# Layer 0 of a four-layer graph network: four gather slots a row, the excess packed over partitions, packing turned round

## The chip, the cores and the metric

The kernel runs on one core of a Trainium2 chip. Its five engines work side by side, each through its own queue in order: TensorE (PE) multiplies matrices, VectorE (DVE) works on rows, ScalarE (ACT) evaluates functions, GpSimd (POOL) here issues indirect DMAs (gathers), SyncE (SP) issues loads. Sixteen DMA engines[...] move data between the large memory (HBM) and the on-chip SBUF; PE writes its sums into PSUM. The metric is the device time of one launch in microseconds, median over the runs.

## The reference, cut to what matters

There are 4096 nodes with 64 features and a 0/1 adjacency with a chance of 1/1024 for each entry, so a row has about four neighbours. Each of four layers adds its output to `x`, on a normalized and rectified copy `h`. Layer 0, which the change concerns, is hyperbolic attention:

```
adj_att = sigmoid(left[:, None] + right[None, :] + b_att) * adj
x_local = logmap(h[:, None, :], h[None, :, :], c)         # per pair (i, j)
support = einsum('ij,ijd->id', adj_att, x_local)
x = x + proj(expmap(h, support, c), c)
```

Only pairs with an edge count, some 16,600 of 16.8 million. Layers 1 and 2 are dense products of the adjacency with features (one, then two), and layer 3 weights each row's last 100 neighbours by powers of one half. These are done as dense matmuls.

## The kernel before, in words

`neighbours` does layer 0, `layers123` the rest. A dense version, `general`, stands behind a flag: it runs only if a row or partition has more neighbours than the lists hold, which these inputs do not.

**Stream.** The adjacency (64 MiB of fp32) comes in 64 pieces of 1 MiB (`load`, L597), eight to a block of 512 rows, through three buffers. From each piece ACT makes an fp8 copy (L774 for the first three blocks, which stay in SBUF; L777 for the others, which go to HBM and come back when layer 1 begins, L1251), and PE packs the bits: 16 adjacency bits of a column become one exactly represented number, with the bit pattern of the piece as the stationary side and an 8-column matrix of powers of two as the moving side (L782). `keys` then holds for each row 256 words with their word numbers in the low bits (added by a matmul of `ones1` and `word_b`, L765; copied by ACT, L788).

**Lists** (`lists`, DVE). For each of the four 128-row tiles of a block the 16 largest words are found (L815 to L817), unpacked into up to 48 candidates, and the `NS` = 7 largest become the row's gather slots (`idx`). What is beyond (`rem`) is collected over 16 tiles; for each partition the `NO` = 12 largest leftovers of such a half are listed with their owners.

**Gathers** (POOL, L890). One indirect DMA fetches one table row (`rows_d`: `h`, its norm terms, the right half of the attention) for each of 128 partitions: 7 for a tile, and for each half 12 neighbours (`es_o`) and 12 owners (`hi_o`).

**Sums.** `chunk` forms the products of neighbours and own rows (L918, L919), `weights` the attention and logmap factor, `sums` scales (L1011) and adds the slots by matmuls with the identity (L1014). `more_sums` spreads each leftover over the tiles of its half, with products on DVE and ACT (L1029, L1027) and 192 matmul records (L1032). `finish` does expmap and projection, eight tiles at a time (L1060 to L1141).

**Order.** All is in a schedule written out by hand: `units_at` says how many pieces to pack at each of 34 items (32 tiles, two overflows), `begin` when lists start, `after` when sums do; `portion` takes turns between the two. Each engine executes in the order of the program.

Of the kernel before, what the change touches and what calls it, by code (L numbers as in the profile page):

```python
# [17 lines left out]
P = 128  # L18
N = 4096
# [23 lines left out]
NS = 7  # L43
GRP = 8
SUP = 16
NO = 12
DQ = D + 1
TW = D + 4
# [526 lines left out]
def neighbours(ctx, tc, x_in, x, sh, adj_t, adj8, a8, over):  # L575
# [5 lines left out]

    nc = tc.nc
# [11 lines left out]
    def load(b, v):  # L594
# [12 lines left out]
    p32_f = l0.tile([P, 1], F32, name="p32_f")  # L607
    G.iota(p32_f, pattern=[[0, 1]], base=0, channel_multiplier=NCH, allow_small_or_imprecise_dtypes=True)
    io16 = l0.tile([P, SUP], F32, name="io16")
    G.iota(io16, pattern=[[1, SUP]], base=1, channel_multiplier=0, allow_small_or_imprecise_dtypes=True)  # L610

    word_b = l0.tile([1, NCH, 8], BF16, name="word_b")
    G.iota(word_b, pattern=[[1, NCH], [NCH, 8]], base=0, channel_multiplier=0, allow_small_or_imprecise_dtypes=True)
    ones1 = l0.tile([1, P], BF16, name="ones1")
    V.memset(ones1, 1.0)

    noff = l0.tile([P, SUP, 16], F32, name="noff")
    G.iota(
        noff, pattern=[[2 * N, SUP], [0, 16]], base=1 - 127 * NCH, channel_multiplier=0,
# [5 lines left out]
    pc_f = l0.tile([P, 1], F32, name="pc_f")  # L625
    cc = l0.tile([P, 8], F32, name="cc")
    wpack = l0.tile([P, 8], BF16, name="wpack")
# [3 lines left out]
    V.tensor_scalar(cc, io16[:, :8], pc_f, None, op0=ALU.is_equal)  # L631
    V.tensor_scalar(pr_i, pr_i, 127 + 8, None, op0=ALU.add)
    V.tensor_scalar(pr_i, pr_i, 23, None, op0=ALU.logical_shift_left)
    V.tensor_scalar_mul(wpack, cc, pr_i.bitcast(F32))
# [49 lines left out]
    left = l0.tile([P, NCH], F32, name="left")  # L684
# [13 lines left out]
    def row_stage(beside):  # L698

        st, var, right = row("st"), row("var"), row("right")  # L700
# [12 lines left out]
        for m in range(NQ):  # L713
            beside()
            V.tensor_mul(cens[m], cens[m], bc(inv[:, rows_of(m)], D))
            S.activation(h[:, rows_of(m), :], cens[m], AF.Relu)
            sq, sr = block(f"sqx{m}"), block(f"sqr{m}")
            S.activation(sq, h[:, rows_of(m), :], AF.Square)
            G.tensor_mul(sr, h[:, rows_of(m), :], sh.wr_t[:, None, :].to_broadcast([P, 8, D]))
            V.tensor_reduce(x2[:, rows_of(m)], sq, AX.X, ALU.add)  # L720
            V.tensor_reduce(right[:, rows_of(m)], sr, AX.X, ALU.add)
            G.tensor_mul(cens[m], h[:, rows_of(m), :], sh.wl_t[:, None, :].to_broadcast([P, 8, D]))
# [15 lines left out]
        V.tensor_scalar(tab[:, :, D + 3], pn, NOISE2, RSQRT_MIN, op0=ALU.mult, op1=ALU.add)  # L738
        V.tensor_sub(la, la, lb)
        V.scalar_tensor_tensor(la, tcl, -2.0, la, op0=ALU.mult, op1=ALU.add)  # L740
        V.tensor_mul(la, la, iv)
        V.tensor_mul(tab[:, :, D + 2], right, la)
        nc.scalar.dma_start(rows_d[1:, :].rearrange("(p n) w -> p n w", p=P), tab)
        return la, cens

    def row_rest(att, cens):
        for m in range(NQ):
            V.tensor_reduce(left[:, rows_of(m)], cens[m], AX.X, ALU.add)
        V.tensor_mul(left, left, att)
        V.tensor_scalar_add(left, left, sh.batt_t)  # L750

        V.tensor_scalar(beta, x2, negc_t, 1.0, op0=ALU.mult, op1=ALU.add)
        V.tensor_scalar_max(clipb, beta, MIN_NORM)
# [4 lines left out]
    def pack(u):  # L758

        b, part = divmod(u, 2)  # L760
        if part == 0:
            keys[b] = l0w.tile([P, 4, NW], F32, tag="keys", bufs=3, name=f"keys{b}")
        pk = psum.tile([P, 4, 16, 8], F32, tag="k", bufs=2, name=f"pk{u}")
        chunks = slice(part * 16, part * 16 + 16)
        T.matmul(  # L765
            pk.rearrange("p k j w -> p k (j w)"), ones1,
            word_b[:, None, chunks, :].rearrange("p k j w -> p k (j w)").to_broadcast([1, 4, 128]),
            start=True, stop=False, skip_group_check=True,
        )
        for v in range(4):  # L770
# [8 lines left out]
            bits = a.bitcast(BF16).rearrange("p j (k i b) -> p j k i b", k=4, b=2)  # L779
            for j in range(4):  # L780
                for k in range(4):
                    T.matmul(  # L782
                        pk[:, k, 4 * v + j, :], bits[:, j, k, :, 1], wpack,
                        start=False, stop=(v == 3 and j == 3), skip_group_check=True,
                    )
            if v < 3:
                yield
        S.copy(keys[b][:, :, part * 128 : part * 128 + 128], pk.rearrange("p k j w -> p k (j w)"))  # L788
# [3 lines left out]
    LB = 4  # L792
# [3 lines left out]
    ovx = [l0.tile([P, NO], U32, name=f"ovx{v}") for v in range(2)]  # L796
    own = [l0.tile([P, NO], U32, name=f"own{v}") for v in range(2)]
    mks = [l0.tile([P, NO], F32, name=f"mk{v}") for v in range(2)]
    rems = {}

    def lists(nb):
        sup, k0 = divmod(nb * LB, SUP)
        nl = LB

# [3 lines left out]
        if k0 == 0:  # L808
            rems[sup] = l0w.tile([P, SUP, 48], F32, tag="rem", name=f"rem{sup}")
        rem = rems[sup]  # L810
        k16 = tile_("k16", [nl, 16])
        scr = tile_("scr", [NW])
        for k in range(nl):
            kk = keys[nb][:, k, :]
            V.max(k16[:, k, :8], kk)  # L815
            V.match_replace(scr, k16[:, k, :8], kk, 0.0)
            V.max(k16[:, k, 8:], scr)  # L817
            yield 1.25
# [5 lines left out]
        ki, wi = tile_("ki", [nl, 16], I32), tile_("wi", [nl, 16], I32)  # L824
        wf, vf = tile_("wf", [nl, 16]), tile_("vf", [nl, 16])
        V.tensor_copy(ki, k16)
        V.tensor_scalar(wi, ki, NW - NCH, 4, op0=ALU.bitwise_and, op1=ALU.logical_shift_left)
        V.tensor_add(wf, wi, noff[:, k0 : k0 + nl, :])
# [6 lines left out]
        cand = tile_("cand", [nl, 3, 16])  # L835
# [9 lines left out]
        j8 = tile_("j8", [nl, 8])  # L845
        for k in range(nl):
# [3 lines left out]
        ji = tile_("ji", [nl, NS], I32)  # L850
# [4 lines left out]
        cr, rm = cand.rearrange("p k l w -> p k (l w)"), rem[:, k0 : k0 + nl, :]  # L855
        V.tensor_tensor(rm, cr, j8[:, :, NS - 1 : NS].to_broadcast([P, nl, 48]), op=ALU.is_lt)
        V.tensor_mul(rm, rm, cr)
        yield 0.9
        if k0 + nl < SUP:
            return  # L860

        ov = l0e.tile([P, 16], F32, tag="ov", name=f"ov{sup}")
        ovm, of = (l0e.tile([P, NO], F32, tag=t, name=f"{t}{sup}") for t in ("ovm", "of"))
        oi, oj = (l0e.tile([P, NO], I32, tag=t, name=f"{t}{sup}") for t in ("oi", "oj"))
        rf = rem.rearrange("p k w -> p (k w)")
        V.max(ov[:, :8], rf)
        yield 1.0
        V.match_replace(rf, ov[:, :8], rf, 0.0)
        yield 1.0
        V.max(ov[:, 8:], rf)  # L870
        V.tensor_copy(flags[:, nb, 2:3], ov[:, NO : NO + 1])
        yield 1.2
        V.tensor_copy(oi, ov[:, :NO])
        V.tensor_scalar(ovm, ov[:, :NO], 0.0, None, op0=ALU.is_gt)
        V.tensor_scalar(oj, oi, 2 * N - 1, None, op0=ALU.bitwise_and)
        yield 0.5
        V.tensor_scalar_min(ovx[sup], oj, N)
        V.tensor_scalar(oj, oi, 13, None, op0=ALU.logical_shift_right)
        V.scalar_tensor_tensor(mks[sup], oj, 1.0, ovm, op0=ALU.add, op1=ALU.mult)
        yield 0.5  # L880
        V.tensor_scalar(of, mks[sup], p32_f, float(SUP * sup), op0=ALU.add, op1=ALU.add)
        V.tensor_mul(of, of, ovm)
        V.tensor_scalar_min(own[sup], of, float(N))
        yield 0.5


    es, s_e, es_o, hi_o, s_o, on_o, w_o = {}, {}, {}, {}, {}, {}, {}
# [6 lines left out]
    def gather(item):  # L894
        kind, n = item
        if kind == "tile":
            g, k = divmod(n, GRP)
            if k == 0:
                es[g] = l0w.tile([P, GRP, NS, TW], F32, tag="es", name=f"es{g}")
            for s in range(NS):  # L900
                fetch(es[g][:, k, s, :], idx[n // LB][:, n % LB, s : s + 1])
            return
        es_o[n] = l0e.tile([P, NO, TW], F32, tag="es_o", name=f"es_o{n}")
        hi_o[n] = l0e.tile([P, NO, TW], F32, tag="hi_o", name=f"hi_o{n}")
        for s in range(NO):
            fetch(es_o[n][:, s, :], ovx[n][:, s : s + 1])
        for s in range(NO):
            fetch(hi_o[n][:, s, :], own[n][:, s : s + 1])

    def chunk(item):  # L910

        kind, n = item
        if kind == "tile":
            g, k = divmod(n, GRP)
            if k == 0:
                s_e[g] = l0w.tile([P, GRP, NS], F32, tag="s_e", name=f"s_e{g}")
            pd = block(f"pd{n}")[:, :NS, :]
            V.tensor_mul(pd, es[g][:, k, :, :D], h[:, n, None, :].to_broadcast([P, NS, D]))  # L918
            V.tensor_reduce(s_e[g][:, k, :], pd, AX.X, ALU.add)  # L919
            return  # L920
        s_o[n] = l0e.tile([P, 1, NO], F32, tag="s_o", name=f"s_o{n}")
        pd = l0e.tile([P, NO, D], F32, tag="pd_o", name=f"pd_o{n}")
# [690 lines left out]
```

## Time and profile before

| | us |
|---|---|
| median of 3 runs | 1254.74 (1245.7 to 2050.95) |
| profiled execution, span | 1141.5 |
| PE busy | 653.3 |
| DVE busy | 547.0 |
| ACT busy | 383.9 |
| POOL busy | 277.3 |

Busy times are sums over the span; the stages differ in what limits them, so each is to be read by itself. A group row gives line, engine, operation, output and input with shapes and a count, then busy time and the mean of one in ns, then the engine's idle time ahead of it and what ended that. A stage row gives busy time and number of instructions of each engine, PE's granted clock (1 is full), the mean busy share of the 16 DMA engines, and GB/s.

### The profile page before, as it was taken

The page shows a single profiled execution, that of the slowest core. Times are in us where ns is not written, and L with a number is a line of the kernel's source. Part 1 is how long each engine was busy: PE and PEld are TensorE (multiplying, and loading weights), DVE is VectorE, ACT ScalarE, POOL GpSimd, SP SyncE. Part 2 cuts the span into 40 slices and gives each one's busy share as a digit, 9 for nine tenths or more (in the row PEclk, how much of TensorE's full clock was granted, in tenths as well). Part 3 has the DMA queues.
Part 4 walks back from the last instruction along what each step waited for, and adds up shares of the span by engine and source line. Part 5 has one row for each costly group of instructions (what it writes and reads, how often), then busy time and mean ns, then how long its engine had stood idle before and what let it go on. Part 6 is the DMA issues. An engine that isn't in the chain of part 4 may idle for free.

```text
span 1141.5 us, 15854 instructions
## 1 busy us (share of the span) xinstructions
PE 653.3 (57%) x6266; PEld 533.8 (47%) x6266; DVE 547.0 (48%) x1599; ACT 383.9 (34%) x576; POOL 277.3 (24%) x290
## 2 busy tenths in 40 slices
PE   1111141033361310434158999899899689999997
PEld 1111030022251210323058999899899556656564
DVE  4762463076848661675643554222244434444443
ACT  4754354036446410533321111111122234334343
POOL 0377765477371766600000000000000000000000
PEclk9999985566575655766569999899999889999999
DMA  8899989857749548200620000000000000000000
GB/s 293 267 312 242 237 246 248 112 119 189 219 118 322 154 20 27 24 0 1 256 113 1 2 1 2 1 1 2 1 2 1 1 1 1 10 1 11 10 1 13
DMA packets 51813, 102.25 MB, mean 90 GB/s; under 512 B 8082, under 2 KB 8082, under 8 KB 50834
## 3 DMA queue, kind: packets, MB, share of 16 engines
q1 hardware_dynamic: 35232, 79.70, 19.9%
q0 software_dynamic: 8704, 9.49, 11.8%
q10 hardware_dynamic: 7794, 11.97, 2.8%
q8 instruction: 51, 0.84, 0.3%
q14 instruction: 32, 0.26, 0.1%
HBM read 88.47 MB, written 12.65 MB: 89 GB/s over the span
## 4 chain that ended last, share of the span: by engine, by line
PE 51%; DVE 15%; DMA 11%; POOL 10%; ACT 6%; issue 6%; ACTq 0%; DVEq 0%; POOLq 0%
PE l2a_acc L1326 8%; PE l_acc L1326 8%; POOL es L890 8%; PE l2b_acc L1326 8%; PE l_acc L1447 7%; PE cnt L1471 6%; PE cnt L1460 5%; DMA hi_o<-rows_d,own 4%; DMA a<-in_adj_t 4%; PE v L1032 4%; PE v L1014 3%; DMA es<-rows_d,idx 2%; POOL es_o L890 2%; ACT f L777 1%; PE l_u L1287 1%
## 5 line engine op out<-in xcount | busy, mean ns | idle before, releaser
L1326 PEld LDWEIGHTS <-a 128*128 128x128 fp8e4 x3072 | 264.4, 99 | 12.5 <-issue 10.5
L890 POOL DMA_INDIRECT es<-rows_d,idx x224 | 219.7, 981 | 132.7 <-issue 86.5
L782 PE MATMUL pk<-wpack,a 128*128 128x8 bf16 x1024 | 36.5, 168 | 196.2 <-DMA a<-in_adj_t 196.2
L1467 DVE TENSOR_SCALAR wt<-cnt 128x512 int16<-128x512 f32 x128 | 88.5, 692 | 122.0 <-PE cnt L1460 122.0
L1468 ACT ACTIVATE wt<-cnt,low_t 128x512 int16<-128x512 f32 x128 | 87.9, 687 | 136.8 <-PE cnt L1460 136.8
L782 PEld LDWEIGHTS <-a 128*128 128x128 bf16 x1024 | 32.0, 103 | 208.0 <-DMA a<-in_adj_t 205.7
L1032 PE MATMUL v<-vo,ident 128*128 128x260 f32 x192 | 55.3, 446 | 113.2 <-DVE vo L1029 109.1
L1447 PE MATMUL l_acc<-y_b,wt 128*128 128x192 bf16 x1024 | 107.2, 248 | 0.0
L1447 PEld LDWEIGHTS <-wt 128*128 128x128 bf16 x1024 | 89.7, 98 | 31.7 <-issue 2.5
L1032 PEld LDWEIGHTS v<-vo,ident 128*128 128x128 f32 x192 | 41.0, 222 | 126.3 <-DVE vo L1029 110.3
L1326 PE MATMUL l_acc<-y_a,a 128*128 128x193 bf16 x1024 | 93.8, 251 | 3.6 <-DVE y_a L1296 3.6
L777 ACT CAST f<-a 128x2048 fp8e4<-128x2048 f32 x40 | 75.8, 1894 | 54.3 <-DMA a<-in_adj_t 49.6
L1014 PE MATMUL v<-es,ident 128*128 128x260 f32 x112 | 40.7, 538 | 88.7 <-DVE es L1011 78.2
L1326 PE MATMUL l2a_acc<-y_b,a 128*128 128x192 bf16 x1024 | 89.1, 249 | 2.9 <-DVE y_b L1296 2.9
L1326 PE MATMUL l2b_acc<-y_a,a 128*128 128x192 bf16 x1024 | 88.1, 248 | 3.0 <-DVE y_a L1296 3.0
L1471 PE MATMUL cnt<-a,fill 128*128 128x512 fp8e4 x248 | 81.3, 384 | 11.1 <-DVE wt L1467 11.1
L1460 PE MATMUL cnt<-a,tri 128*128 128x512 fp8e4 x256 | 78.4, 388 | 9.6 <-DVE tri L1440 9.6
L1014 PEld LDWEIGHTS v<-es,ident 128*128 128x128 f32 x112 | 30.3, 278 | 96.5 <-DVE es L1011 89.6
L774 ACT CAST a<-a 128x2048 fp8e4<-128x2048 f32 x24 | 45.3, 1894 | 31.5 <-DMA a<-in_adj_t 29.9
L1027 ACT ACTIVATE vo<-es_o,on 128x65 f32<-128x65 f32 x128 | 32.8, 337 | 64.0 <-PE v L1032 61.3
L1460 PEld LDWEIGHTS <-tri 128*128 128x128 bf16 x256 | 24.8, 97 | 47.0 <-issue 22.1
L923 DVE TENSOR_TENSOR pd_o<-es_o,hi_o 128x768 f32<-128x768 f32 x2 | 1.9, 966 | 79.6 <-DMA es<-rows_d,idx 79.6
(333 smaller groups left out, 799.1 us busy)
## 6 DMA issues: line engine op xcount, KB each, us to landing
a<-in_adj_t SPq DMA_DIRECT2D x64, 1024.0 KB, 9.5
adj<-f ACTq DMA_DIRECT2D x40, 256.0 KB, 6.6
a<-adj SPq DMA_DIRECT2D x5, 2048.0 KB, 21.5
es<-rows_d,idx POOLq DMA_INDIRECT x224, 6.0
rows_d<-tab ACTq DMA_DIRECT2D x1, 1088.0 KB, 4.7
x<-in_x SPq DMA_DIRECT2D x1, 1024.0 KB
out<-z SPq DMA_DIRECT2D x4, 256.0 KB, 2.0
es_o<-rows_d,ovx POOLq DMA_INDIRECT x24, 7.7
```

Of the source, the lines that this page charges most:

```text
L774: S.copy(a8[b][:, 4 * at : 4 * at + 4, :], a, saturate=False)
L777: S.copy(f8, a, saturate=False)
L782: T.matmul(pk[:, k, 4 * v + j, :], bits[:, j, k, :, 1], wpack, start=False, stop=(v == 3 and j == 3), skip_group_check=True,)
L890: G.indirect_dma_start(out=dst, out_offset=None, in_=rows_d, in_offset=bass.IndirectOffsetOnAxis(ap=at, axis=0))
L1014: T.matmul(pv, sh.ident, es[g][:, 4 * q : 4 * q + 4, s, :DQ], start=(s == 0), stop=False, skip_group_check=True,)
L1032: T.matmul(banks[g][:, half, : 4 * DQ], sh.ident, vo[:, 4 * q : 4 * q + 4, :].rearrange("p k e -> p (k e)"), start=False, stop=(s == NO - ...
L1326: T.matmul(acc, a8[n // 4][:, c, n % 4 * P : (n % 4 + 1) * P], y3[:, c, :cols], start=(c == first[0] and k % 2 == 0), stop=(c == last[-1] ...
L1447: T.matmul(accs[k // 2][:, k % 2, : 3 * D], wts[k // 4][:, (k % 4) * P : (k % 4 + 1) * P].bitcast(BF16), y3[:, c, : 3 * D], start=(c == NC ...
L1460: T.matmul(cnt[b], tri, masks[b], start=head_, stop=last, skip_group_check=True)
L1467: V.tensor_scalar(wts[0], cnt[0], -(128.0 - MAX_NEIGH) * UNIT, 0.0, op0=ALU.add, op1=ALU.max)
L1468: S.activation(wts[1], cnt[1], AF.Relu, bias=low_t)
L1471: T.matmul(cnt[b], fill, masks[b], start=False, stop=False, skip_group_check=True)
```

## The change

Layer 0 is written anew on the same idea.

- A row has four slots instead of seven. What is beyond is no longer kept with its own partition: within each block, every partition lists up to 24 leftovers (`NV`), a matmul with a strict triangle (`before`) counts those of the partitions ahead of it, and a second matmul with a 0/1 matrix (`mine`) moves each leftover to its place in a list of 4 × 128 (`NO`). So a block needs 16 + 4 neighbour gathers and 4 owner gathers.
- A leftover's contribution is added to its row by a matmul with a 0/1 matrix (`spot`), in place of `more_sums`.
- Packing has the adjacency as moving side: 4 matmuls of 512 columns for a piece, with 128-column windows of a wide `wpack` as stationary side. The result lies with words on partitions, so ACT adds the numbers as a bias and PE transposes each 128 × 128 part into `keys`, which is in PSUM now.
- The table row has one word more (the left half of the attention), so this is computed before the table is written.
- The order comes from a loop that keeps a clock of its own: it packs a piece when it should have arrived, runs lists before anything else, then products of blocks whose gathers should have landed, then sums and finishes.
- In the later layers, the triangle masks of layer 3 are made before layer 1, one product is placed two chunks earlier, and a buffer count is written as an expression.

```diff
-NS = 7
-GRP = 8
-SUP = 16
-NO = 12
+NS = 4
+LB = 4
+NV = 24
+NO = 4
-TW = D + 4
+TW = D + 5
...
-            keys[b] = l0w.tile([P, 4, NW], F32, tag="keys", bufs=3, name=f"keys{b}")
-        pk = psum.tile([P, 4, 16, 8], F32, tag="k", bufs=2, name=f"pk{u}")
+            keys[b] = [psum.tile([P, 2, NW], F32, tag="k", bufs=2, name=f"keys{b}_{s}") for s in range(2)]
+        pk = psum.tile([P, 512], F32, tag="pk", bufs=2, name=f"pk{u}")
...
             for j in range(4):
-                for k in range(4):
-                    T.matmul(
-                        pk[:, k, 4 * v + j, :], bits[:, j, k, :, 1], wpack,
-                        start=False, stop=(v == 3 and j == 3), skip_group_check=True,
-                    )
+                w = 4 * v + j
+                T.matmul(
+                    pk, wflat[:, w * P : (w + 1) * P], bits[:, j, :, 1], start=(w == 0), stop=(w == 15),
+                )
...
+        kt = l0w.tile([P, 512], F32, tag="kt", name=f"kt{u}")
+        S.activation(kt, pk, AF.Identity, bias=num[:, part : part + 1])
+        for k in range(LB):
+            T.transpose(
+                keys[b][k // 2][:, k % 2, part * P : part * P + P], kt[:, k * P : (k + 1) * P], sh.ident
+            )
...
+        for v in range(0, NV, 8):
+            V.max(ov[:, v : v + 8], rf)
+            if v + 8 < NV:
+                V.match_replace(rf, ov[:, v : v + 8], rf, 0.0)
...
+        T.matmul(pb[:, :1], before, cnb, start=True, stop=True)
...
+        V.tensor_scalar(from_, io, at0, None, op0=ALU.is_gt)
+        V.tensor_add(end, at0, cnt)
+        V.scalar_tensor_tensor(mine, io, end, from_, op0=ALU.is_le, op1=ALU.mult)
...
+        for c in range(NO):
+            T.matmul(pe[:, c, :], mine[:, c * P : (c + 1) * P], mv, start=True, stop=True, skip_group_check=True)
...
+            for c in range(NO):
+                V.tensor_scalar(spot[:, c, :], io, rows_at[nb][:, c : c + 1], None, op0=ALU.is_equal)
+                yield 0.4
+            ek = es[g][:, q, :, :DQ]
+            V.tensor_mul(ek, ek, bc(w[:, q - q0, :], DQ))
...
+            for c in range(NO):
+                for k in range(LB):
+                    T.matmul(
+                        pv[:, k * DQ : (k + 1) * DQ], spot[:, c, k * P : (k + 1) * P],
+                        es[g][:, q, LB * NS + c, :DQ], start=False, stop=(c == NO - 1 and k == LB - 1),
+                        skip_group_check=True,
+                    )
...
+    PACE_MB, PACE_DMA, LANDED, SLOW = 3.6, 1.27, 8.0, 1.1
...
+        def can_pack():
+
+            b, v = divmod(packed[0], 8)
+            return b < NR and (v < 3 or turned[0] >= b)
...
+        arrived = [38.0 + PACE_MB * (m - 8) for m in range(8 * NR)]
...
+        follow = {
+            1: [sums(0, 0, 2), finish(0, 0, 8)],
+            3: [sums(1, 0, 2), finish(1, 0, 8)],
+            5: [sums(2, 0, 2), finish(2, 0, 8)],
+            6: [sums(3, 0, 1)],
+            7: [sums(3, 1, 2), finish(3, 0, 8)],
         }
...
+            while can_pack() and arrived[packed[0]] <= now + 1.0:
+                pack_one()
+            job = None
+            if listed < NR and packed[0] >= 8 * (listed + 1):
+                job = todo[listed]
+            elif pending and pending[0][1] <= now and (pending[0][0] < 4 or pending[0][0] // 2 * 2 - 3 in summed):
+                job = pending[0][2]
+            elif side:
+                job = side[0]
...
-                if q == 0 and c == 20:
+                if q == 0 and c == 22:
                     third_y(0)
```

## The prediction

> **What bounds the kernel now.** I read the page first, for where the engines are dense, then the same span cut into stages, then the chain of waits, then the queue waits. The page's second part:
>
> ```profile
> PE   1111141033361310434158999899899689999997
> DVE  4762463076848661675643554222244434444443
> POOL 0377765477371766600000000000000000000000
> PEclk9999985566575655766569999899999889999999
> DMA  8899989857749548200620000000000000000000
> GB/s 293 267 312 242 237 246 248 112 119 189 219 118 322 154 20 27 24 0 1 256 113 1 2 1 2 1 1 2 1 2 1 1 1 1 10 1 11 10 1 13
> ```
>
> A slice is 28.5 us. From slice 21 on PE is dense: layers 1 to 3, which the change hardly touches. Before it, for half of the span, no engine is dense for long; that is layer 0. The stages of layer 0:
>
> ```profile
> core 0: us, PE busy (x) PEld busy (x) DVE busy (x) ACT busy (x) POOL busy (x), PEclk, DMA share, GB/s
> 0.00:57.00 57.00, 9.24 (x196) 6.44 (x196) 34.68 (x115) 34.68 (x34) 11.63 (x18) 1.00 0.85 280
> 57.00:126.00 69.00, 10.45 (x243) 7.87 (x243) 35.13 (x126) 30.94 (x20) 51.06 (x54) 1.00 1.00 276
> 126.00:205.00 79.00, 17.21 (x239) 13.48 (x239) 31.41 (x103) 32.93 (x25) 47.30 (x49) 0.73 0.90 230
> 205.00:290.00 85.00, 19.39 (x178) 15.22 (x178) 44.52 (x158) 33.84 (x57) 57.97 (x60) 0.60 0.72 150
> 290.00:384.00 94.00, 33.29 (x305) 25.15 (x306) 64.09 (x222) 52.29 (x71) 43.16 (x44) 0.59 0.75 226
> 384.00:480.00 96.00, 27.50 (x122) 21.34 (x122) 45.19 (x146) 18.77 (x48) 65.73 (x68) 0.62 0.48 28
> 480.00:552.00 72.00, 21.35 (x64) 15.21 (x64) 48.78 (x213) 26.64 (x59) 0.44 (x1) 0.62 0.01 1
> ```
>
> Up to 126 us the DMA engines are full. From 205 on they have holes although adjacency is still to come: its last piece is cast at 383 us. From 384 to 480 POOL is the busiest (68 gathers), then DVE alone. Layer 0 ends at 552 us, where the readback of the fp8 blocks is issued (551.98). DVE is busy 304 of these 552 us. Why the stream has holes stands in the chain and in the load queue's waits:
>
> ```profile
> 194.25 15.54 DMA hi_o<-rows_d,own
> 210.04 15.99 DMA hi_o<-rows_d,own
> ...
> 434.38 11.75 DMA hi_o<-rows_d,own
> 446.39 7.06 DMA es<-rows_d,idx
> ```
>
> ```profile
> SPq L597 <- PE pk L782: 212.1, 40, 48.0
> ```
>
> A half's overflow is gathered in one lump of 24, DVE and then PE wait for it, and the packing matmuls behind it on PE's queue hold the load buffers: the loads waited 212 us for L782, once for 48 us. One row of groups gives POOL's price:
>
> ```profile
> L890 POOL DMA_INDIRECT es<-rows_d,idx x224 | 219.7, 981 | 132.7 <-issue 86.5
> ```
>
> In a row of gathers the starts are 1.25 us apart (0.94 busy, 0.30 issue).
>
> [...] loads without gathers come every 3.2 us (casts from 55.6 to 71.7), with 28 gathers beside eight loads every 4.4 us (71.7 to 106.9). [...]
>
> **The change part by part.**
>
> *Gathers.* Before: 224 + 24 + 24 = 272. After: 8 blocks of 16 + 4 + 4 = 192. POOL: 192 × 1.25 = 240 us, 30 us a block, never the bound while a block's transfer takes longer than that. Lumps go, since each block gathers its own excess.
>
> *Packing.* Before 16 matmuls of 8 columns a piece; after 4 of 512 columns. The fp8 512-column pair in layer 3 takes 0.43 us at full clock (L1460), so 0.215 each, 0.43 at half clock: 1.7 us a piece, plus per half block one Identity on ACT (the copy it replaces took 0.58) and four transposes (about 0.3 to 0.4 each, from L1274's 1.09 for four). A moving operand with a 4-byte stride is not in the trace; if it cost double, 3.4 us. ACT's cast is 1.9 a piece. A piece takes 3.2 to 5.3 us to arrive: hidden, either way.
>
> *Lists, on DVE, per block.* Key search 4 × (412 + 92 + 409 + 428 ns) = 5.4 us; flags and unpacking 1.9; three levels 3 × 0.89 = 2.7; the flag of the last level, L847, and the indices 0.2 + 0.8 + 0.5; remainder 0.7. Up to here, with the rest of the old list, 12.2. New: three searches and two replacements over 192 elements (between the 195 ns of 48 and the 412 of 256 wide: about 0.36 each, 1.9); some 23 small operations at 0.19 = 4.4; two 512-wide masks at 0.43 to 0.69 = 1.3; three operations of 96 to 192 elements, 1.0. Sum 20.8, taken as 21. Reading keys from PSUM instead of SBUF is not shown; a 512-wide read of PSUM (L1467) takes 0.69, as a two-input one of SBUF does, so nothing is added.
>
> *Per block after that.* Products and their reduction: L918 and L923 (448: 624 ns; 768: 966) extrapolate to 1.24 for 1024, 0.43 for 256 and 1.5 for the reduction: 3.2. Weights of two blocks at 40 columns: between 5.7 us (28 wide, 517.2 to 522.9) and 6.5: 6.0. Per block four 512-wide spots at 0.43 (the fp32 one-input form of L1550) and one product of 1300 elements (from L1011's 631 for 455: 1.7) = 3.4. Finish of eight tiles: 476.2 to 494.7 less the products lying in it = 16.0.
>
> DVE would need 50 us for the row stage and 8 × 21 + 8 × 3.2 + (3 × 12.8 + 18) + 4 × 16 = 314, so 364 us at the least. It is not the bound if the stream is slower.
>
> *The stream.* Bytes up to the last piece: 67.1 MB adjacency, 1.0 x, 1.1 table, 10.5 fp8 copies, 168 gathers of 128 rows of 276 bytes = 5.9; together 85.7. The first 57 us moved 16.0. The other 69.7 MB go at what full engines showed: 276 GB/s with 0.78 gathers a us (57 to 126), 289 from 330 to 384 us at a share of 0.92; with 0.67 gathers a us I take 287. 69.7 / 0.287 = 243, so the last piece lands at 300 us (309 at 276).
>
> *What then is left.* The new order is fixed by a planner that expects a piece every 3.6 us and puts lists ahead of all else. Added up from its portions, between two blocks it leaves room for only some 5 to 8 us of other work. So when the last block's lists begin, the products of blocks 0 to 3 and most of the first sums are done, and behind them stand: rest of sums 0 (1.5), products 4 to 7 (12.8), three more sums (12.8 + 12.8 + 18) and four finishes (64): 122 us of DVE in one chain. No load hides it. Each finish also waits for PE: per block 4 fp32 matmuls of 260 columns (0.75 at half clock: two records of 0.38) and 16 of 65 columns whose two weight loads take 0.2 each (L1032) = 3 + 6.4 = 9.4 us. For the four finishes that leaves, after what DVE does beside it, about 3, 11, 10 and 7 = 31 us (half that at full clock, 45 if weights and columns don't overlap). 122 + 31 = 153.
>
> *Sum.* 300 + 5 (casts, transposes) + 21 (lists 7) + 153 = 479 against 552: 73 us less. The block's own gathers (16 × 1.25 after 13 us of lists, packed ones done some 53 us after the last piece) lie under the first 85 us of the tail.
>
> *At no cost.* Moving the left sums ahead of the table adds 2.7 + 0.4 us to the row stage while the DMA queue fills. Building the triangle masks early adds 1.2 us before layer 1 and takes 0.6 before layer 3, where PE waits 9.6 us for a chain in which they are last. Third-product placement (22 for 20) reorders equal work. The buffer expression gives the same counts (2 and 1).
>
> The timed runs are 111 us above the profiled one (1254.74 to 1143.31). The trace doesn't say why; I carry it over whole. 1254.7 − 73 = 1182.
>
> **The rivals.** *B, gathers ride free* (chance 0.22): DMA cost of a gather vanishes between long transfers, a piece comes every 3.6 us. For: the packets' own times, 2.85 us a MB for loads, give 231 us without gathers. Against: 4.4 against 3.2 us a load above. The last piece at 236: 236 + 26 + 153 = 415, 1118 us[...].
> *C, lockstep, slower* (0.08): queues are in order; a planner faster than the real stream puts the next block's packing behind list matmuls on PE that wait for DVE, and the buffers (three) stop the loads. For: the 212 us above. Against: list work of 21 us lies under a 35 to 42 us transfer. If nothing overlapped for seven blocks, 7 × 21 = 147 more: 626, that is 1329.
> *D, no difference* (0.15): stream at 255 GB/s (330 us) and a tail of 190, with doubled PE waits and table loads: 546, 1249. For: 230 GB/s from 126 to 205 us. Against: that stage had the 28 us hold of PE in it.
>
> **How the numbers follow.** The main case has 0.55. B adds 0.22 and a fifth of D lies above 2%: faster 0.80; same 0.12; slower 0.08 from C. [...]
>
> **What would show it.** Right: DMA share near 1 up to about 300 us, the last cast there, no load wait for packing over 10 us; then a stretch of 150 to 180 us with DMA nearly empty, DVE above two thirds busy, waits of finish on PE of some 10 us. B: last cast by 245. C: load-queue waits on PE or ACT in every block. Wrong altogether: last cast near 384 as before, or DVE idle in the tail on table loads. The dense layers should keep their length within 2 us[...].

## The result, and the profile after

The changed kernel takes 1185.11 us (1179.12 to 1188.52, four runs), the kernel before 1251.33 in the same comparison: a ratio of 0.948, 95% interval 0.9412 to 0.9548. The ratios compare fast runs alone, so runs over 1.5% above the fastest of their kernel are left out, here one of the kernel before at 2050.95 us and later two of e3's four. The forecast was 1182. The time is right by luck: the experiments below show two steps of the sum wrong by nearly the same amount in opposite directions. The second part of the changed kernel's page, as slices of the span:

```profile
PE   3453334456210040042226899899989779999997
DVE  5746455776601622266554545422144434444443
POOL 0375566000067127500000000000000000000000
PEclk9856556565565565565657999899999979999999
DMA  8788797996011001100080000000000000000000
GB/s 293 246 283 278 231 303 258 336 344 241 9 21 29 7 9 28 21 1 0 1 351 5 2 1 2 1 2 1 2 1 2 1 1 1 9 2 9 4 7 12
```

A slice is 29.7 us. DMA is busy for ten slices and then nearly empty, as forecast. What was not forecast stands on the other rows: POOL stops in slices 8 to 11, where it has nothing in its way that the sum knew of, and the second half of layer 0 has slices in which neither PE, DVE nor DMA does much. Part of the same span by stages:

```profile
core 0: us, PE busy (x) PEld busy (x) DVE busy (x) ACT busy (x) POOL busy (x), PEclk, DMA share, GB/s
57.00:126.00 69.00, 30.58 (x90) 11.15 (x90) 37.80 (x171) 33.01 (x20) 41.96 (x45) 0.60 0.84 273
290.00:384.00 94.00, 18.25 (x88) 15.15 (x87) 23.83 (x91) 3.84 (x9) 39.76 (x42) 0.54 0.11 18
384.00:480.00 96.00, 13.33 (x80) 12.20 (x80) 37.44 (x117) 16.28 (x29) 40.28 (x43) 0.55 0.10 16
480.00:597.00 117.00, 27.24 (x160) 24.42 (x160) 61.87 (x239) 26.65 (x45) 11.33 (x13) 0.60 0.03 4
```

From 290 to 597 us DVE, which was to be the chain, is busy 123 of 307 us. POOL gathers again from 331 to 392 and from 435 to 495 us, after the adjacency stream has ended. What it waited for, among POOL's waits:

```profile
POOL es L934 <- PE v L1065: 170.6, 2, 127.4
```

Its timeline has the two places, with the wait before each in brackets:

```profile
203.43 0.94 POOL L934 DMA_INDIRECT hi<-rows_d,own  x1 [0.30 <-issue]
331.74 0.94 POOL L934 DMA_INDIRECT es<-rows_d,idx  x1 [127.37 <-PE v L1065]
...
434.93 0.94 POOL L934 DMA_INDIRECT es<-rows_d,idx  x1 [43.23 <-PE v L1065]
```

`es` and `hi` have two buffers, and each holds two blocks of rows. The gathers of blocks 4 and 5 need the buffer of blocks 0 and 1, which comes free with the last matmul of the first sums (L1065). The written-out order puts those sums behind the last block's lists, and in this profile all records of PE (5602), DVE (1705) and ACT (468) and POOL's 192 gathers stand in the order of the program. So 48 gathers of 1.25 us start at 331.7 instead of near 205, and the next 48 wait for the second sums. DVE's waits show who pays:

```profile
DVE pd L965 <- DMA es<-rows_d,idx: 78.5, 3, 32.2
DVE pd L977 <- DMA hi<-rows_d,own: 18.9, 2, 9.6
DVE pd L977 <- issue: 9.6, 1, 9.6
```

All three rows are the first products of the gathered rows, between 324 and 467 us, and together 107 us (the third has no releaser named, but stands in the same place as the second). Note what hides the cause here: DVE's row names the DMA, and the DMA is nearly idle (a share of 0.11 and 0.10 from 290 to 480 us). Only POOL's row, one step further back, names the buffer. Layer 0 ends at 597.2 us, where the readback L1262 is issued; the span is 1186.5.

### The profile page after: what moved, and what is told of

Its sections match the earlier page's. It is cut to its first block, busy times and chain, and to the rows that moved or that the text cites. A ratio compares the mean times of both kernels' runs of the same rounds, so it can differ in the third digit from the quotient of the medians.

```text
span 1186.5 us, 14354 instructions
## 1 busy us (share of the span) xinstructions
PE 699.4 (59%) x5602; PEld 527.3 (44%) x5602; DVE 550.2 (46%) x1705; ACT 347.9 (29%) x468; POOL 194.2 (16%) x208
## 5 line engine op out<-in xcount | busy, mean ns | idle before, releaser
L785 PE MATMUL pk<-a,wpack 128*128 128x512 bf16 x256 | 110.4, 582 | 106.0 <-DMA a<-in_adj_t 79.5
L934 POOL DMA_INDIRECT es<-rows_d,idx x128 | 122.7, 959 | 248.5 <-PE v L1065 170.6
L1059 PE MATMUL v<-es,ident 128*128 128x260 f32 x64 | 26.3, 581 | 215.8 <-issue 208.1
L1479 DVE TENSOR_SCALAR wt<-cnt 128x512 int16<-128x512 f32 x128 | 88.5, 691 | 122.5 <-PE cnt L1472 122.5
L1059 PEld LDWEIGHTS v<-es,ident 128*128 128x128 f32 x64 | 17.9, 294 | 221.1 <-issue 208.5
L785 PEld LDWEIGHTS <-wpack 128*128 128x128 bf16 x256 | 32.4, 131 | 180.6 <-issue 166.5
L965 DVE TENSOR_TENSOR pd<-es,tab 128x1024 f32<-128x1024 f32 x8 | 9.8, 1226 | 79.5 <-DMA es<-rows_d,idx 78.5
L793 PE MATMUL keys<-ident,kt 128*128 128x128 f32 x64 | 17.4, 425 | 39.6 <-ACT kt L791 22.7
L1483 PEld LDWEIGHTS <-fill 128*128 128x128 bf16 x248 | 24.2, 98 | 28.0 <-issue 21.3
L1065 PEld LDWEIGHTS v<-es,spot 128*128 128x128 f32 x256 | 34.6, 216 | 1.1
```

What stands on the lines that cost most here:

```text
L785: T.matmul(pk, wflat[:, w * P : (w + 1) * P], bits[:, j, :, 1], start=(w == 0), stop=(w == 15),)
L934: G.indirect_dma_start(out=dst, out_offset=None, in_=rows_d, in_offset=bass.IndirectOffsetOnAxis(ap=at, axis=0))
L1059: T.matmul(pv.rearrange("p (k e) -> p k e", k=LB), sh.ident, slots[:, s], start=(s == 0), stop=False, skip_group_check=True,)
L1065: T.matmul(pv[:, k * DQ : (k + 1) * DQ], spot[:, c, k * P : (k + 1) * P], es[g][:, q, LB * NS + c, :DQ], start=False, stop=(c == NO - 1 an ...
L1479: V.tensor_scalar(wts[0], cnt[0], -(128.0 - MAX_NEIGH) * UNIT, 0.0, op0=ALU.add, op1=ALU.max)
L1483: T.matmul(cnt[b], fill, masks[b], start=False, stop=False, skip_group_check=True)
```

## The experiments

The kernels were run in three jobs, each on one chip, with the kernel before timed in each: job 1 (e1 to e4), where it takes 1261.31 us; job 2 (e5 to e8), where it takes 1140.34; job 3 (e9 to e12), where it takes 1249.35. Ratios are to the kernel before of the same job.

**e1: the kernel before once more, unchanged.** The forecast carried 111 us between the first profile of the kernel before (span 1141.5) and its timed runs.

> The kernel before, unchanged, profiled anew. Theory A: the one profile at 1141.5 us was an unusually short execution of the kernel before, and the timed runs near 1250 us are its usual length; then this profile has a span near 1245 us, the dense layers still take 589 us, and layer 0 takes about 655 us in place of 552. Theory B (the prediction's step): a profiled execution is about 111 us shorter than a timed one of the same kernel; then the span is near 1141 us again while the time beside it is near 1250 us.

This profiled execution took 1261.63 us. Layer 0 ends at 670.3 (551.98 in the first profile), the rest takes 589.5 (589.5). So the 111 us are no cost of timing or profiling: they lie in layer 0, and there they show. PE's timeline in the first profile and in this one, in the same stretch:

```profile
75.94 0.59 PE L782 MATMUL pk<-wpack,a 128*128 128x8 bf16 x16 [3.62 <-DMA a<-in_adj_t]
82.60 0.59 PE L782 MATMUL pk<-wpack,a 128*128 128x8 bf16 x16 [6.06 <-DMA a<-in_adj_t]
```

```profile
80.16 0.17 PE L782 MATMUL pk<-wpack,a 128*128 128x8 bf16 x1 [1.23 <-issue]
82.25 0.17 PE L782 MATMUL pk<-wpack,a 128*128 128x8 bf16 x1 [1.93 <-issue]
82.97 0.17 PE L782 MATMUL pk<-wpack,a 128*128 128x8 bf16 x1 [0.56 <-issue]
```

Sixteen matmuls in one go after a wait for data in the first; one at a time in the second, with gaps in which PE waits for nothing that the profile shows (`issue`). Those shown stand inside a piece, whose data are there. In e1 they sum to `PE pk L782 <- issue` 103.3 us in 62 gaps; in the first profile that row is absent. The loads wait for the buffers (73.2 us for L782, 80.1 for ACT's casts), and DMA moves 195 GB/s from 57 to 126 us where the first profile has 276.

**e2: a third buffer for `es` and `hi`.**

```diff
-            es[g] = l0w.tile([P, 2, NE, TW], F32, tag="es", name=f"es{g}")
-            hi[g] = l0w.tile([P, 2, NO, TW], F32, tag="hi", name=f"hi{g}")
+            es[g] = l0w.tile([P, 2, NE, TW], F32, tag="es", bufs=3, name=f"es{g}")
+            hi[g] = l0w.tile([P, 2, NO, TW], F32, tag="hi", bufs=3, name=f"hi{g}")
```

> The changed kernel with three buffers in place of two for the gathered rows (es and hi); nothing else. Theory A: after the last piece, layer 0 is held by this ring: gathers of blocks 4 and 5 wait for the first sums, those of 6 and 7 for the second, and POOL's 171 us of waiting come out almost whole. Then the gathers of blocks 4 and 5 run beside the stream, the last cast moves from 298 to at most 310 us, layer 0 ends near 490 us in place of 597, and the time falls by about 105 us to 1080. Theory B: the tail is the DVE chain and PE's waits, and the moved gathers slow the stream by as much as they save; the time stays within 20 us of 1185.

1108.13 us, ratio 0.8781 (0.8731 to 0.8831). The changed kernel stands at 0.948 in its own comparison and 0.9439 in e10, so one buffer is worth 0.066 to 0.070 of the kernel before, some 85 us: theory A, with less than the 105 us expected. POOL waits for a buffer once, 64.0 us, and the 107 us of DVE's waits for gathered rows shrink to 3.1. Layer 0 ends at 526.1. The last cast is later (314.5 for 298.3), since 48 more gathers now share the stream: 16.2 / 48 = 0.34 us each, if all of the delay is theirs. That is rough, because the changed kernel's own last cast comes at 289.8 in e10, 8.5 us earlier. From the end of the last lists (339) the tail is now 187 us for the 153 forecast, and most of the rest is one term of that sum, DVE's first operation of the finish, which waits for PE's sums, copied out of PSUM by ACT (31 forecast). Among DVE's waits:

```profile
DVE f_t L1091 <- ACT vs L1071: 51.8, 4, 30.5
```

**e3: the turned packing alone, put into the kernel before.** The slots, lists and gathers stay as they were.

```diff
-                for k in range(4):
-                    T.matmul(
-                        pk[:, k, 4 * v + j, :], bits[:, j, k, :, 1], wpack,
-                        start=False, stop=(v == 3 and j == 3), skip_group_check=True,
-                    )
+                w = 4 * v + j
+                T.matmul(
+                    pk, wflat[:, w * P : (w + 1) * P], bits[:, j, :, 1], start=(w == 0), stop=(w == 15),
+                )
```

> The kernel before with the packing alone turned round (adjacency as moving side, 4 matmuls of 512 columns a piece, numbers added by ACT, four transposes, one more copy from PSUM so that lists read SBUF as before). Theory A: packing lies under the arrival of a piece; the time stays within 10 us of the kernel before. Theory B: PE's packing time (about 0.58 us for each of 256 matmuls as the changed kernel shows it) lengthens the hold of the load buffers; layer 0 and the time grow by 25 us or more. Theory C: the turned packing is what makes the changed kernel faster; the time falls by 30 us or more.

Ratio 0.9711 (0.9651 to 0.977), 36 us; the median of all four runs, 1233.98, is only 27 us below the kernel before. So theory C's 30 us are met or nearly so. The trace, of a run of 1241.41 us, still has gaps: 33.7 us of `issue` in 12 before the packing, for 103.3 in 62 in e1.

**e4: three buffers, and the planner told that a piece takes longer,** so that more of the sums falls between the lists.

```diff
-    PACE_MB, PACE_DMA, LANDED, SLOW = 3.6, 1.27, 8.0, 1.1
+    PACE_MB, PACE_DMA, LANDED, SLOW = 4.4, 1.27, 8.0, 1.1
```

> Three buffers as before, and the planner's clock expects a piece every 4.4 us in place of 3.6 (the changed kernel's last cast near 285 us gives 4.4 on average), so that the first finish and the first part of the second sums come before the last block's lists. Theory A: the work moved ahead fills holes of DVE in the stream, and the tail shrinks by the 16 + 2 us of the first finish and what it waits for, 20 to 25 us against three buffers alone. Theory B: the fixed order then ties packing to work that is late, the stream ends later by as much, and nothing is gained (within 8 us).

1103.29 us, ratio 0.8748 (0.8711 to 0.8786), which is not told apart from e2's. POOL waits for no buffer any more, but the last cast moves from 314.5 to 362.0, and DVE still waits 48.8 us in four finishes. PE's waits for the counts of the lists (L876), which stand ahead of later packing in PE's queue, grow from 40.4 to 88.5 us. So what the order gives to the tail it takes from the stream, which is theory B.

**e5: three buffers, that pace, and each finish one group later than its sums.**

```diff
-            1: [sums(0, 0, 2), finish(0, 0, 8)],
-            3: [sums(1, 0, 2), finish(1, 0, 8)],
-            5: [sums(2, 0, 2), finish(2, 0, 8)],
+            1: [sums(0, 0, 2)],
+            3: [sums(1, 0, 2), finish(0, 0, 8)],
+            5: [sums(2, 0, 2), finish(1, 0, 8)],
...
-            7: [sums(3, 1, 2), finish(3, 0, 8)],
+            7: [sums(3, 1, 2), finish(2, 0, 8), finish(3, 0, 8)],
```

> Three buffers and a pace of 4.4 us a piece as in the run before, and each finish placed behind the next sums (first finish after the second sums, second after the third, last two at the end). Theory A: the waits of finish for PE, 49 us in the run before (prediction: 31 us), are covered by the sums that now lie between; the time falls by 25 to 40 us, to about 1070. Theory B: the end of layer 0 is set by gathers and the stream, not by this chain; the time stays within 8 us of 1103.

1025.09 us, ratio 0.9007 (0.8949 to 0.9066); layer 0 ends at 431.2, and the finishes' waits for sums are gone from DVE's list. The 1070 expected were meant for the chip of job 1, and three edits differ from the changed kernel at once, so this run doesn't price the lag by itself.

**e6: the changed kernel with two buffers, and e4's line of `PACE_MB` 4.4 as its only edit.**

> The changed kernel with its two buffers, pace of 4.4 us in place of 3.6, so that the first sums are done before the lists of block 5 and free the first buffer while the stream runs; the second sums still end behind the last lists. Theory A (the ring): POOL's wait of 127 us for the first sums falls to near nothing and only the second wait stays; most of what three buffers gave comes back, about 1115 to 1140. Theory B (three buffers helped for another reason, such as more slack between products and gathers): the time stays near 1185.

1072.86 us, ratio 0.9404 (0.9351 to 0.9458), 69 us less than e8 below. The first sums come earlier and give the buffer back earlier: POOL's two waits for it are 92.6 us together, where e8 has 153.4. The first wait doesn't fall to near nothing, as theory A had it (the longer of the two is 61.8), and the pace moves other work too, so the buffer is not tested alone here.

**e7: the changed kernel with the old packing, and e8: the changed kernel unchanged.** In e7 sixteen matmuls of 8 columns a piece come back, with keys copied to SBUF, and all else of the change stays.

```diff
-                w = 4 * v + j
-                T.matmul(
-                    pk, wflat[:, w * P : (w + 1) * P], bits[:, j, :, 1], start=(w == 0), stop=(w == 15),
-                )
+                for k in range(4):
+                    T.matmul(
+                        pk[:, k, 4 * v + j, :], bits[:, j, k, :, 1], wpack[:, 0, :8],
+                        start=False, stop=(v == 3 and j == 3), skip_group_check=True,
+                    )
```

> The changed kernel with the old packing (adjacency as stationary side, 16 matmuls of 8 columns a piece, word numbers by a matmul, keys copied by ACT to SBUF); all else as changed. Theory A: PE gets instructions too slowly for 16 matmuls and 16 weight loads a piece while gathers run; the one-by-one matmuls of the kernel before come back, the last cast moves from 298 to 320 us or later and the time rises by 20 to 60 us to 1205 or more. Theory B: those stalls came from the overflow lumps of the kernel before, not from the packing; the time stays within 10 us of 1185.

> The changed kernel, unchanged, on the same chip as the three others, as their base: 1185 us within 1%, layer 0 ending near 597 us of the profile, POOL waiting some 170 us for the sums.

e7 took 1135.16 us, ratio 0.9959 (0.9936 to 0.9982). e8 took 1142.17, ratio 1.0018 (0.9989 to 1.0047): on this chip the change makes no difference, and its turned packing costs 7 us. Both expectations are missed, since the base itself is not at 1185 here. The stage from 57 to 126 us in e8, in e7, and then in e1:

```profile
57.00:126.00 69.00, 38.71 (x112) 14.14 (x114) 53.65 (x239) 41.26 (x29) 48.62 (x52) 0.60 1.02 350
57.00:126.00 69.00, 15.44 (x340) 11.31 (x340) 55.38 (x243) 40.96 (x29) 48.58 (x51) 1.00 1.04 363
```

```profile
57.00:126.00 69.00, 9.98 (x189) 7.30 (x189) 22.16 (x76) 24.60 (x16) 44.51 (x47) 1.00 0.70 195
```

In e8 the DMA engines are full and PE's `issue` waits before the packing are 1.1 us; e7 has none at all. The last cast comes at 255.0, 43 us sooner than in the first profile of the changed kernel and 128 sooner than in that of the kernel before (383). Yet layer 0 ends only at 548.1 (551.98 there): all that the stream gains the tail loses, because POOL waits for the buffers just the same:

```profile
POOL es L934 <- PE v L1065: 153.4, 2, 106.5
```

**e9 to e12: the same four questions on a third chip.** The kernel before (e9), the changed kernel (e10), the old packing in it as in e7 (e11), e5's kernel (e12).

> The kernel before, unchanged. Theory A (two kinds of executions that go by the chip): either layer 0 ends near 552 us with no one-by-one packing matmuls and a span near 1141, or it ends near 670 with TensorE's packing matmuls losing about 100 us in 'issue' gaps and a span near 1260; the dense rest takes 589 to 590 either way. Theory B (a drift that spreads over the program): a dense rest that differs by over 5 us, or a span in between with both parts longer.

> The changed kernel, unchanged. Theory A: where the kernel before takes about 1255 in the same job, a ratio of 0.94 to 0.955; where it takes about 1140, a ratio of 0.99 to 1.01. Theory B (the change is worth the same everywhere and the earlier job was odd): 0.94 to 0.955 with either.

> The changed kernel with the old packing (one matmul for each 128 columns, the adjacency stationary) and everything else of the change kept. Theory A (many small packing instructions cost only where instructions come late): where the kernel before takes about 1255, 15 to 60 us slower than the changed kernel in the same job, with 'issue' gaps before TensorE's packing matmuls; where it takes about 1140, within 10 us of it. Theory B (the way of packing doesn't matter anywhere): within 10 us with either.

> Three buffers for the wide gathers' targets, column blocks due at 4.4 us a MB, and sums and finishes that follow one block later. Theory A: 1020 to 1060 whatever the kernel before takes, since it neither waits for buffers nor issues many small packing instructions: a ratio near 0.90 where that takes 1140, near 0.82 to 0.85 where it takes 1255. Theory B (it gains a fixed share): a ratio of 0.895 to 0.907 with either.

e9: 1243.71 us, layer 0 ends at 652.7, the rest takes 589.2, and the packing has 68.9 us of `issue` gaps: theory A, with smaller gaps than expected. e10: 1182.51, ratio 0.9439 (0.9381 to 0.9498). e11: 1213.17, ratio 0.9687 (0.963 to 0.9744). Both are as theory A has it: here the old packing costs 31 us where in job 2 it saved 7, and the gaps are there. First PE's `issue` waits before the packing in e11 and in e10, then a piece of e11's timeline, then one of e10's in which the same work is four wide matmuls:

```profile
PE pk L795 <- issue: 71.1, 49, 3.1
```

```profile
PE pk L785 <- issue: 21.6, 10, 4.1
```

```profile
78.30 0.24 PE L795 MATMUL pk<-wpack,a 128*128 128x8 bf16 x3 [3.11 <-issue]
79.93 0.21 PE L795 MATMUL pk<-wpack,a 128*128 128x8 bf16 x2 [1.39 <-issue]
80.63 0.17 PE L795 MATMUL pk<-wpack,a 128*128 128x8 bf16 x1 [0.49 <-issue]
```

```profile
77.41 1.86 PE L785 MATMUL pk<-a,wpack 128*128 128x512 bf16 x4 [0.91 <-issue]
80.33 1.86 PE L785 MATMUL pk<-a,wpack 128*128 128x512 bf16 x4 [1.05 <-issue]
```

A gap in e10 stands ahead of four matmuls, in e11 ahead of one to three. e12 misses its expectation: 1092.37 us, ratio 0.8721 (0.867 to 0.8772), where 1020 to 1060 was expected. It has few small packing instructions and waits for no buffer, and still its last cast comes at 356.1 (e5: 294.6), with `issue` gaps before its packing of 28.8 us (e5: 0.7) and waits of PE for the counts of the lists of 83.2 (48.1). Wide packing does away with most gaps inside a piece (57.3 us in e11, none in e10, 7.1 in e12), not with those ahead of one (13.8, 21.6, 21.7).

## Why the time was right and the sum was not

**Where the two errors lie.** The forecast had layer 0 end at 479, the rest 589 and 111 of offset. The first profile of the changed kernel has 597.2, 589.3 and none (its span of 1186.5 is what it is timed at). The end of layer 0 is 118 us late, the offset 111 us too much: +7 together, and the median is 3 us off the forecast.

**The offset: failed.** "The timed runs are 111 us above the profiled one ... I carry it over whole." The step that failed is to take the offset for a cost of timing that every kernel pays. It belonged to the executions: the first profile of the kernel before is like those of job 2 (1140), its timed runs are like those of jobs 1 and 3 (1250 to 1261). A gain read between that profile and a sum built on it was a gain for the first kind. There 73 us were forecast, and the measured gain is nothing (e8).

**The stream: the number held, the working did not.** Last piece forecast at 300, last cast at 298.3; 273 GB/s from 57 to 126 us for the 287 taken. But in e8, an execution of the kind that the rate was read from, the last cast is at 255.0, and the DMA engines carry 350 GB/s beside 52 gathers. The sum had two terms too large for that kind. It had 168 gathers beside the stream; in both traces only 96 were issued before the last cast, since the others waited for buffers. And it took the price of a gather from the kernel before. The gathers' queue in the first profile of the kernel before, and in that of the changed kernel (packets, MB, time of the packets as a share of 16 engines' span):

```profile
q0 software_dynamic: 8704, 9.49, 11.8%
```

```profile
q0 software_dynamic: 6144, 6.80, 3.4%
```

With 272 and 192 gathers this gives an estimate of 0.118 × 1141.5 / 272 = 0.50 us of all 16 engines for a gather before, and 0.034 × 1186.5 / 192 = 0.21 after. In e5, where 162 of the 192 run beside the stream, it is 0.19 (3.5% of 1023.9 us). Why a gather became cheaper isn't shown. In the first profile of the changed kernel the stream is slower than in e8 for another reason (see "What stays open"), so that it ended where the forecast had it by luck. Rival B, gathers that ride free, is not out: its sign was a last cast by 245, and e8 comes near. Rival C, lockstep, is out by the time of the last cast, but PE does wait 28.5 us in five places for the counts of the lists. The sign "no load wait for packing over 10 us" isn't met cleanly: waits that name the packing reach 8.0 us (48.0 before), but eight more, `SPq L599 <- remote: 58.4, 8, 15.7`, name no releaser (SPq is SyncE's queue).

**The tail: failed, and this is the step that mattered.** "The block's own gathers ... lie under the first 85 us of the tail" took it that a block's gathers can start when its indices are there. The list of costs had a price for each of the 192 gathers and none for the buffer that they write to. After the last lists (323 us) the tail took 597 − 323 = 274 us for the 153 forecast; 107 of the 121 too much are DVE's waits for those gathers. In e8, with its faster stream, the tail is as long (from about 280 to 548 us). DVE is busy 123 of 307 us where two thirds were expected. e2 takes most of the cause away (POOL waits 64.0 us in place of 170.6) and 85 us with it. Waits for PE in the finishes were forecast at 31 us; with the buffer wait in front they are 18.2, without it (e2) 51.8.

**Small terms: held.** Products 1.23 + 0.42 + 1.49 = 3.1 us a block (3.2 forecast), four packing matmuls 1.86 (1.7), lists of the last block 302 to 323 (21), a POOL start every 1.25 us, dense rest 589.3 (589).

**What the change is worth, part by part.** Job 3 splits it: all but the packing 1249.35 to 1213.17, 36 us; the turned packing 31 more. e3 gives the packing alone 36 us in job 1 (27 by the median of all its runs). In job 2 the same steps give 5 us and then take 7. In both kinds the waits for buffers take from what the change gains; with e5's kernel the gain comes out in both, 115 us (0.9007) in job 2 and 157 (0.8721) in job 3. How much of that is the lag of the finishes alone isn't settled: e12's ratio is not told apart from that of e4, which has no lag.

**What stays open.** Shown is that sixteen small matmuls a piece cost 31 us more than four wide ones on one chip (e11 against e10) and 7 us less on another (e7 against e8), and that the first pair differs in gaps, 71.1 us against 21.6. Counted in the traces, these rows hold two kinds. Inside a piece, ahead of a matmul that waits for no semaphore, e11 has 57.3 us in 43 gaps and e1 has 86.6 in 54; e10 has none, e7 none, and e12, with wide packing too, 7.1 in seven. So this kind goes with small matmuls on the chips of jobs 1 and 3. Ahead of a piece, where a wait for data whose signal isn't on record would look the same, e11 has 13.8 us and e10 all of its 21.6. What makes either is not shown. That instructions come late to the engine, as theory A of e7 and of e11 has it, is an argument: for the first kind no wait is on record, and the same program on another chip lacks it (71.1 us in e11, none in e7). Nor are PE's instructions all that is late. In the first profile of the changed kernel, PE's packing and then the next loads:

```profile
193.71 3.62 PE L785 MATMUL pk<-a,wpack 128*128 128x512 bf16 x8
198.62 1.06 PE L785 MATMUL pk<-a,wpack 128*128 128x512 bf16 x4 [1.29 <-issue]
```

```profile
208.21 1.47 SPq L599 DMA_DIRECT2D a<-in_adj_t  x3
```

These are the last three pieces that had come; ACT had cast them by 200.6 us, so all three load buffers were free. Still the three loads are issued only from 208.21 us on, and DMA moves 55 GB/s from 200 to 208 us. So the signal that frees a buffer may be late as well as an instruction; no run tells the two apart. Each chip was used in one job only, and what differs between the chips is not known.

## What to carry to other kernels

Price a buffer as you price an instruction: for each transfer of a new stage, ask which instruction frees its target and where the written-out order puts that one; when an engine waits long for a DMA that is idle, look one step back, at what the issuing engine waits for; here it was a buffer. A difference between the profiled and the timed run is to be located, by profiling again, before it is carried into a sum. And where small instructions come with gaps between them, try fewer and wider ones: in job 3 they paid 31 us, though PE's busy time rose from 13.04 (e11) to 32.36 (e10) of the 69 us from 57 to 126.

## What the runs showed of the hardware that was not expected

The kernel before takes 1136 to 1147 us (23 runs) on one chip and 1247 to 1263 (14 runs) on two others. In its three profiles, one short and two long, what follows layer 0 takes 589.2 to 589.5 us, so all of the difference lies in layer 0. The granted clock doesn't explain it: from 57 to 126 us it is 1.00 in the first profile, which takes 1143.31 us, and in e1, which takes 1261.63.

Nor did the granted clock follow PE's busy time. In the first profiles of both kernels each record of it is 1.00 or 0.50, the full and the half clock of the prediction; the kernel before has 0.50 from 210 to 215 us and a mean of 0.96 from 906 us on, where L1460 stands. From 57 to 126 us its PE is busy 10.45 of 69 us and is granted 1.00, from 290 to 384 us 33.29 of 94 and 0.59. In the stage shown above, e7's PE is busy 15.44 of 69 us with small matmuls and is granted 1.00, and e8's is busy 38.71 with wide ones and is granted 0.60. What decides it isn't shown.

A packing matmul whose moving side has a stride of 4 bytes over 512 columns cost little more than estimated from dense rows: in the first profile of the changed kernel four in 1.86 us (1.7 forecast) where the granted clock was 0.50 (187.7 to 189.6 us), and in 1.06 where it was 1.00 (198.6 to 199.7).
